# A four-layer vision kernel on one core: layer 3's bias tables built by DRAM-to-DRAM copies, and activation groups placed behind ready decays

## The chip, the cores and the metric

The kernel runs on one core of a Trainium2 chip. The metric is the device time of one execution in microseconds (us), lower is better. Engines are named as in the profile: PE (TensorE), DVE (VectorE), ACT (ScalarE), POOL (GpSimd) and SP (SyncE, which here only issues DMAs). Everything is fp32.

## The reference, cut to what matters

Four images of 64 x 64 positions and 128 channels go through four layers, image by image independently.

```python
# layer 0: state-space scan block (256 inner channels, 16 states, 4 directions)
xn = _ln(input); x_, z = split(xn @ in_proj_w)
xc = silu(depthwise_conv3x3(x_) + conv_b)
xs = stack([x0, x1, x0[..., ::-1], x1[..., ::-1]])       # rows, columns, and both reversed
delta = softplus(dts + dt_b); A = -exp(A_log)
h = exp(d_t * A) * h + (d_t * x_t) * B_t                  # scan over 4096 positions
y_t = einsum('bkdn,bkn->bkd', h, C_t)
x = input + (_ln(y) * silu(z)) @ out_proj_w
x = x + gelu(_ln(x) @ fc1_w + fc1_b) @ fc2_w + fc2_b
# layer 1: attention over all 4096 positions; layer 2: convolutions with hard-swish
# layer 3: attention of each position over its 7 x 7 neighbourhood, 4 heads
bias = rpb[:, rel_i][..., rel_j]
attn = softmax(einsum('nhijc,nhiajbc->nhijab', q, kwin) + bias)
x = x + attn_out @ proj_w + proj_b
x = x + gelu(_ln(x) @ fc1_w + fc1_b) @ fc2_w + fc2_b
```

## The kernel before, in words

**The scan.** `selective_scan` (L457 on) handles one image at a time: four directions, eight chunks of 512 positions, two halves, four groups of states, two pairs. The innermost step, a *unit*, works on a tile `[128, 2, 512]`. POOL makes `dB` = du x B (L504). For each of two halves g, ACT makes the decay `dA` = exp(delta x A) into a PSUM bank (L510; three banks in turn), and DVE scans along the positions (L512). The product with C (`hc`, into which PE sums at L558) is made by POOL for a fixed part of the units (L525; 5 of 16 for image 0, 7 of 16 for the others, `ON_POOL`), else by DVE in two halves (L517). There are 2048 units and so 4096 decays, 1024 to an image. The inputs `dt`, `du`, `b_rows` and `c_rows` come from DRAM through SP's queue, with four buffers each.

**What feeds it.** `scan_inputs` (L277) runs once for each image: LayerNorm, projection, the 3 x 3 convolution and silu chunk by chunk, then for both orders of positions the softplus on ACT and the product `du` on POOL (L328), all stored in DRAM. Image 0's inputs come first; those of images 1, 2 and 3 follow beside image 0's scan.

**What follows it.** `rest` runs the later stages of one image beside the scan of the next: `scan_output` (end of layer 0 with its MLP; its first product on DVE is `gated`, L626), `layer1`, `layer2` and `layer3_attention` (its product `oT` on DVE, L1387, comes once for each of eight chunks). The second half of layer 3, `layer3_mlp`, runs beside the next image's `scan_output`. Image 3's `rest` has the core to itself.

**What orders the work.** Nothing is ordered by hand. A scheduler puts each engine's instructions in an order when the kernel is built, by priorities and by its own estimate of when an instruction is ready; a lower number goes first. The scan has `SCAN_FIRST`, 10,000,000, and the other stages count up from zero, so they go ahead of it. On the chip each engine then keeps that order. SBUF pools are reused stack-wise: a stage that opens a pool waits until the memory's last user is done.

**Groups.** ACT's exp and ln share one function table; gelu and silu need others. The class `Together` (L100) puts the gelus or silus of one step in a row: each waits for the step's last matmul, all have a priority of -100 x `SCAN_FIRST`, and `exp_table` (L93) then loads the exp table back at once. There are 100 groups, of four activations nearly always.

**The bias tables.** `make_bias` (L1187) builds T, `[128, 52, 64]`: for each key column, head and row distance the bias at every query column, or -10000 outside of the window. It then builds 12 tables of 1 MB for three kinds of chunk. For each it fills a tile `bt` with -10000 on DVE (L1240), copies three or so row ranges out of T (L1251, SBUF to SBUF) and stores `bt` to DRAM (L1252). There is one `bt` buffer, so each memset waits for the store before it. The pool of T and `bt` is freed after that, and the scan inputs of image 1 use the memory next. `layer3_attention` loads the tables much later (L1325).

Of the kernel before, what the change touches and what calls it, by code (L numbers as in the profile page):

```python
# [28 lines left out]
F32 = mybir.dt.float32  # L29
# [14 lines left out]
NCH = NT // LC  # L44
# [10 lines left out]
BEHIND = 2  # L55
ON_POOL = ((1, 4, 7, 10, 13), (0, 2, 4, 6, 9, 11, 13))
SCAN_FIRST = 10_000_000

# [7 lines left out]
def mid(ap, n):  # L68

    return bc(ap.unsqueeze(1), [ap.shape[0], n, ap.shape[1]])  # L70
# [6 lines left out]
@contextmanager  # L77
def priority(tc, K, base):

    kept = tc.cur_priority  # L80
    tc.cur_priority = K.next_priority.get(base, base)
    yield
    K.next_priority[base] = tc.cur_priority
    tc.cur_priority = kept
# [15 lines left out]
class Together:  # L100
# [8 lines left out]
            after(self.tc, matmul, self.done)  # L109

    def run(self, last_matmul, acts):
        with priority(self.tc, self.K, -100 * SCAN_FIRST):
            for act in acts:
                self.done = act()
                after(self.tc, self.done, last_matmul)
        exp_table(self.tc, self.K, self.done)


# [941 lines left out]
def key_kind(c):  # L1060
    return 0 if c == 0 else 2 if c == NCH - 1 else 1
# [122 lines left out]
    nc.vector.tensor_scalar(K.bounds[0:1, 0, 7:8], top[:, 0:1], -1.0, 1.0, ALU.mult, ALU.add)  # L1184


def make_bias(tc, K, A, out):  # L1187

    nc = tc.nc
    NR = 2 * KW - 1
    NQ = 9
    with ExitStack() as ctx:
        pool = ctx.enter_context(tc.tile_pool(name="bias", bufs=1))
        psum = ctx.enter_context(tc.tile_pool(name="bias_p", bufs=4, space=PSUM))
        rp = loader(tc, pool, A, 3)("rpbT", [NR, HEADS * NR])

        shifted = pool.tile([NR, 2 * W], F32, name="shifted")
        nc.gpsimd.memset(shifted, 0.0)  # L1200
        nc.gpsimd.affine_select(
            shifted, shifted, [[1, 2 * W]], ALU.not_equal, 1.0, base=KW - W, channel_multiplier=-1
        )
        dist = pool.tile([128, W], F32, name="dist")
        kj = pool.tile([128, W], F32, name="kj")
        for i in range(2):
            half = slice(64 * i, 64 * i + 64)
            for t, pattern, base in ((dist, [[-1, W]], KW - 1), (kj, [[0, W]], 0)):
                nc.gpsimd.iota(
                    t[half, :], pattern, base=base, channel_multiplier=1, allow_small_or_imprecise_dtypes=True  # L1210
                )
        low = pool.tile([128, W], F32, name="low")
        high = pool.tile([128, W], F32, name="high")
        t = pool.tile([128, W], F32, name="t")
        nc.vector.tensor_scalar(low, dist, float(KW // 2), None, ALU.is_ge)
        nc.vector.tensor_scalar(t, kj, float(W - KW), None, ALU.is_ge)
        nc.vector.tensor_max(low, low, t)
        nc.vector.tensor_scalar(high, dist, float(KW - 1 + KW // 2), None, ALU.is_le)
        nc.vector.tensor_scalar(t, kj, float(KW - 1), None, ALU.is_le)
        nc.vector.tensor_max(high, high, t)  # L1220
        nc.vector.tensor_mul(low, low, high)
        nc.vector.tensor_scalar(low, low, -1.0, -FAR, ALU.add, ALU.mult)
        T = pool.tile([128, HEADS * NR, W], F32, name="T")
        for q0 in range(0, W, NQ):
            n = min(NQ, W - q0)
            ps = psum.tile([128, NQ, HEADS * NR], F32, name="ps")
            for q in range(n):
                first = W - 1 - q0 - q
                for i in range(2):
                    nc.tensor.matmul(  # L1230
                        ps[64 * i : 64 * i + 64, q, :], shifted[:, first : first + W], rp, start=True, stop=True
                    )
            nc.vector.tensor_add(
                T[:, :, q0 : q0 + n], ps[:, :n, :].rearrange("p q e -> p e q"), mid(low[:, q0 : q0 + n], HEADS * NR)
            )
        T4 = T.rearrange("p (h r) w -> p h r w", h=HEADS)
        for c in (0, 1, NCH - 1):
            for i, group in enumerate(key_groups(c)):
                bt = pool.tile([128, HEADS, RC, W], F32, name="bt")
                nc.vector.memset(bt, FAR)  # L1240
                for tile_, q0, q1, at in group:
                    for r in range(2):
                        key, half = 2 * tile_ + r, slice(64 * r, 64 * r + 64)
                        rows = [
                            q for q in range(q0, q1)
                            if 0 <= key - min(max(RC * c + q - KW // 2, 0), H - KW) < KW
                        ]
                        if rows:
                            n, to = len(rows), at + rows[0] - q0
                            far = KW - 1 - key + RC * c + rows[0]  # L1250
                            nc.sync.dma_start(bt[half, :, to : to + n, :], T4[half, :, far : far + n, :])  # L1251
                nc.sync.dma_start(out[key_kind(c)][i], bt.rearrange("p h r w -> p h (r w)"))  # L1252


def layer3_attention(tc, K, A, D, img, wide, out=None):
# [445 lines left out]
def network(tc, A, out):  # L1701
    nc = tc.nc
    with ExitStack() as ctx:
        nc.scalar.preload_act_table_set("natural_log_exp_and_others")
        K = make_consts(ctx, tc)
        dram = ctx.enter_context(tc.tile_pool(name="scratch", bufs=1, space=DRAM))

        def scratch(name, shape):
            return dram.tile(shape, F32, name=f"{name}_dram")

        D = SimpleNamespace()
        D.bias = scratch("bias", [len(BIAS_KINDS), 128, HEADS * 512])
        D.biasT = [[scratch(f"biasT{k}_{i}", [128, HEADS, LC]) for i in range(4)] for k in range(3)]
        D.conv_diag = scratch("conv_diag", [128, ND, 9, 128])
        D.w2_norms = scratch("w2_norms", [128, len(NORMS2), 4])
        D.w2_cv4, D.w2_bias = scratch("w2_cv4", [128, 128]), scratch("w2_bias", [1, 128])
        for name, shape in (("sz", [128, ND, LC]), ("xc", [128, ND, LC]), ("y", [128, ND, LC])):
            setattr(D, name, [[scratch(f"{name}{b}_{c}", shape) for c in range(NCH)] for b in range(B)])
        for name, shape in (("delta", [128, ND, LC]), ("du", [128, ND, LC]), ("bc", [NS, 2, LC])):
            made = [  # L1720
                [[scratch(f"{name}{b}_{k}_{c}", shape) for c in range(NCH)] for k in range(KD)] for b in range(B)
            ]
            setattr(D, name, made)
        D.y_first = [[[scratch(f"y_first{b}_{k}_{c}", [128, ND, LC]) for c in range(NCH)] for k in range(2)] for b in range(B)]
        D.y_cols = [scratch(f"y_cols{b}", [NCH, 128, NCH, ND, RC * RC]) for b in range(B)]
        for name in ("x4", "x5"):
            setattr(D, name, [scratch(f"{name}_{b}", [NT, C]) for b in range(B)])
        D.shift = [scratch(f"shift{b}", [NJ, 128]) for b in range(B)]

        with ExitStack() as scan_ctx:  # L1730
            S = make_scan(scan_ctx, tc, K, A)
            make_conv_diagonals(tc, K, A, D.conv_diag)
            with priority(tc, K, SCAN_FIRST // 2):
                with tc.tile_pool(name="mk_w2", bufs=1, side="right") as pool:
                    make_layer2(tc, K, A, D, pool)
            scan_inputs(tc, K, A, D, 0)
            before = None
            for img in range(B):
                with priority(tc, K, SCAN_FIRST):
                    selective_scan(tc, K, S, D, img)  # L1740
                if img == 0:
                    make_bias(tc, K, A, D.biasT)
                    for later in range(1, B):
                        scan_inputs(tc, K, A, D, later)
                    more = scan_ctx.enter_context(tc.tile_pool(name="ss_more", bufs=1))
                    S.products.widen(more, 4)
                    S.inputs.widen(more, 1)
                else:
                    rest(tc, K, A, D, img - 1, before)
                    before = img - 1, out[img - 1]  # L1750
            rest(tc, K, A, D, B - 1, before, scan_ctx.close, out[B - 1])
        needed = ctx.enter_context(tc.tile_pool(name="needed", bufs=1)).tile([1, 1], mybir.dt.int32, name="needed")
        bound_exceeded(tc, K, needed)
        with tc.If(nc.values_load(needed) > 0):
            everything_again(tc, K, A, D, out)
# [80 lines left out]
```

## Time and profile before

| what | us |
|---|---|
| median of three runs (lowest, highest) | 8791.7 (8789.48, 8803.95) |
| the profiled execution | 8797.75 |
| its span in the trace | 8795.8 |
| busy in the span: DVE, POOL, PE, ACT | 7141.1, 7049.4, 6999.8, 5683.3 |
| last decay (L510) starts | 7592.9 |
| first `gated` (L626) of image 3 | 7753.1 |

A line of groups gives source line, engine, operation, tiles (out<-in), shapes and count, then after the bar the busy time in us, the mean duration of one in ns, and after the next bar the time that the engine was idle just before them, with what ended it. A line of windows gives the stretch, its length, the busy us and instruction count of PE, PEld (weight loads), DVE, ACT and POOL, the granted PE clock, the share of the DMA engines' time that was busy, and GB/s. In the line of 40 slices each digit is a busy share in tenths.

### The profile page before, as it was taken

The numbers are of one execution on the slowest core, as the hardware profiler recorded it, in microseconds if no ns is written. First come the engines' busy times: TensorE is split into PE (matmuls) and PEld (weight loads), VectorE is DVE, ScalarE is ACT, GpSimd is POOL, SyncE is SP. The second block draws the span as 40 slices with busy tenths as digits, with TensorE's granted clock in tenths as the row PEclk, the third lists the DMA queues.
The fourth block names the chain that finished last, engine by engine and source line by source line (L and its number), as shares of the span: only waits on it lengthen the run. The fifth ranks groups of instructions, "written<-read, shape, count | busy, mean of one in ns | idle before, by whom it ended". The sixth has DMA issues, their size and how long they took to land. (4 is left out here: it accounts for less than half of the span.)

```text
span 8795.8 us, 102113 instructions
## 1 busy us (share of the span) xinstructions
PE 6999.8 (80%) x30532; PEld 2613.9 (30%) x30532; DVE 7141.1 (81%) x8531; ACT 5683.3 (65%) x11661; POOL 7049.4 (80%) x3079
## 2 busy tenths in 40 slices
PE   6844858687679897887789987777799888788988
PEld 2211313132332222333322222233322223344333
DVE  4789878787899999998899999998899999513433
ACT  5645767676566676666766676667766676454366
POOL 6888999989889999998899999998899999500000
PEclk8756868787789998898899988898899988899989
DMA  5777777777655556566555557565455565320020
GB/s 178 242 235 240 246 252 236 268 245 256 194 168 172 169 175 213 193 217 196 164 175 170 175 167 233 194 217 183 155 177 173 180 215 195 108 70 5 1 82 12
DMA packets 855473, 1572.02 MB, mean 179 GB/s; under 512 B 218341, under 2 KB 336764, under 8 KB 851197
## 3 DMA queue, kind: packets, MB, share of 16 engines
q1 hardware_dynamic: 724605, 1389.21, 48.1%
q10 hardware_dynamic: 130304, 176.19, 5.7%
q8 instruction: 244, 4.00, 0.2%
q14 instruction: 320, 2.62, 0.1%
HBM read 1273.92 MB, written 280.18 MB: 177 GB/s over the span
## 5 line engine op out<-in xcount | busy, mean ns | idle before, releaser
L504 POOL TENSOR_TENSOR dB<-du,b_rows 128x1024 f32<-128x1024 f32 x2048 | 4835.5, 2406 | 416.0 <-DVE hc L512 112.3
L510 ACT ACTIVATE dA<-dt,w_A_log 128x512 f32<-128x512 f32 x4096 | 2781.3, 690 | 481.7 <-DVE hc L512 217.8
L512 DVE TENSOR_TENSOR_SCAN dA<-dA,state,dB 128x512 f32<-128x512 f32 x2128 | 2629.6, 1272 | 273.8 <-POOL dB L504 134.9
L525 POOL TENSOR_TENSOR hc<-hc,c_rows 128x1024 f32<-128x1024 f32 x832 | 2003.9, 2409 | 64.4 <-ACT state L521 29.1
L512 DVE TENSOR_TENSOR_SCAN hc<-dA,state,dB 128x512 f32<-128x512 f32 x1456 | 1804.3, 1267 | 148.2 <-ACT dA L510 110.5
L517 DVE TENSOR_TENSOR hc<-dA,c_rows 128x512 f32<-128x512 f32 x2432 | 1563.6, 675 | 92.1 <-PE py L558 60.5
L558 PE MATMUL py<-hc,pick 128*32 128x512 f32 x8192 | 1231.5, 682 | 383.4 <-POOL hc L525 294.3
L519 ACT COPY state<-dA 128x1 f32<-128x1 f32 x2128 | 326.7, 159 | 1292.1 <-DVE hc L517 1281.8
L848 PE MATMUL pa<-e,l_v 128*128 128x512 f32 x2048 | 1061.4, 650 | 14.4 <-ACT e L804 12.5
L800 PE MATMUL pair<-l_g,l_f 32*128 32x512 f32 x2048 | 528.0, 664 | 169.9 <-ACT e L804 141.0
L988 POOL MEMSET l_h<- 64x128 f32 x8 | 2.1, 256 | 811.6 <-DVE l_h L962 811.6
L804 ACT ACTIVATE e<-pair 128x1024 f32<-128x1024 f32 (+1 forms) x448 | 508.4, 1135 | 221.0 <-PE pair L800 213.7
L848 PEld LDWEIGHTS pa<-e,l_v 128*128 128x128 f32 x2048 | 374.8, 199 | 666.1 <-issue 620.4
L558 PEld LDWEIGHTS py<-hc,pick 128*32 128x32 f32 x8192 | 209.9, 116 | 1148.2 <-issue 472.5
L247 PE MATMUL ps<-band,w_conv_diag 128*128 128x504 f32 (+3 forms) x1152 | 500.2, 594 | 6.0 <-ACT delta L397 5.6
L1354 PE MATMUL pair<-table,ident 128*128 128x512 f32 x768 | 400.4, 646 | 100.1 <-ACT e L1364 72.9
L512 DVE TENSOR_TENSOR_SCAN dA<-dA,dB 128x512 f32<-128x512 f32 x304 | 355.9, 1211 | 62.2 <-POOL dB L504 51.7
L201 PE MATMUL ps<-ident,ln_xn 128*128 128x128 f32 x512 | 136.5, 363 | 316.3 <-ACT ln_xn L198 251.6
L328 POOL TENSOR_TENSOR du<-delta,xc 128x1024 f32<-128x1024 f32 x128 | 334.6, 2622 | 56.6 <-ACT delta L397 50.1
L1364 ACT ACTIVATE e<-pair 128x1024 f32<-128x1024 f32 (+1 forms) x224 | 254.6, 1137 | 161.5 <-PE pair L1358 160.9
L247 PEld LDWEIGHTS ps<-band,w_conv_diag 128*128 128x128 f32 x1152 | 221.4, 193 | 285.0 <-issue 262.6
L800 PEld LDWEIGHTS pair<-l_g,l_f 32*128 32x128 f32 x2048 | 139.0, 188 | 518.7 <-ACT e L804 284.0
(285 smaller groups left out, 8709.7 us busy)
## 6 DMA issues: line engine op xcount, KB each, us to landing
b_rows<-bc_dram SPq DMA_DIRECT2D x1024, 256.0 KB
c_rows<-bc_dram SPq DMA_DIRECT2D x1024, 256.0 KB
dt<-delta_dram SPq DMA_DIRECT2D x512, 512.0 KB
du<-du_dram SPq DMA_DIRECT2D x512, 512.0 KB
delta_dram<-delta ACTq DMA_DIRECT2D x128, 512.0 KB
du_dram<-du SPq DMA_DIRECT2D x128, 512.0 KB
table<-biasT_dram SPq DMA_DIRECT2D x72, 512.0 KB
y_first_dram<-y_sum ACTq DMA_DIRECT2D x128, 256.0 KB
```

The source lines that it names most:

```text
L247: mm = nc.tensor.matmul(out[:, r0 - row0 : r1 - row0, c0:c1], lhsT((dy + 1) * 3 + dx + 1), src[:, r0 + dy : r1 + dy, c0 + dx : c1 + dx], s ...
L328: nc.gpsimd.tensor_mul(du.rearrange("p d (a b) -> p d a b", b=H), deltas[b].rearrange("p d (a b) -> p d a b", b=H), tk,)
L504: nc.gpsimd.tensor_mul(dB, dus[pp], mid(bt, 2))
L510: nc.scalar.activation(dA, dts[pp][:, g, :], AF.Exp, scale=S.A[:, k, j, pr, g : g + 1])
L512: nc.vector.tensor_tensor_scan(hg[:, order], dA[:, order], dB[:, g, order], 0.0 if i == 0 else state[:, j, pr, g : g + 1], ALU.mult, ALU.add,)
L517: mm = nc.vector.tensor_mul(hc[:, g, :], dA, ct)
L525: made.append(nc.gpsimd.tensor_mul(hc, hc, mid(ct, 2)))
L558: mm = nc.tensor.matmul(py[0][32 * q : 32 * q + 32, :], S.pick, hcs[q // 2][:, q % 2, :], start=(k == 1 and j == 0), stop=(j == NJS - 1),)
L800: nc.tensor.matmul(ps[:, u, :], f[quad, t // 4, span(t % 4, 128)], g[quad, c, :], start=True, stop=True)
L804: made = nc.scalar.activation(e, ps, AF.Exp)
L848: nc.tensor.matmul(pa, v[:, 8 * q + t, :], es[q], start=(t == 0 and q == 0), stop=(t == 7 and q == 3),)
L1354: nc.tensor.matmul(ps[:, u, :], K.ident, t[:, u, :], start=True, stop=False)
```

## The change

Two things. First, T gets one more row that holds -10000 throughout, and is stored to DRAM (`D.T`). The 12 tables are put together from there by DMAs whose source and destination are both in DRAM: one for each run of rows that follow each other in T, and one for each row that lies outside of the window. These DMAs are issued from `place_bias`, after the pool is closed and with the priority `LAST` x `SCAN_FIRST`, behind everything else. `bt`, its memsets and its copies are gone. Second, the first activation of a group gets that same last priority, and the others follow it with the old one.

```diff
+LAST = 50
...
     def run(self, last_matmul, acts):
-        with priority(self.tc, self.K, -100 * SCAN_FIRST):
-            for act in acts:
+        first = None
+        for act in acts:
+            with priority(self.tc, self.K, (LAST if first is None else -100) * SCAN_FIRST):
                 self.done = act()
                 after(self.tc, self.done, last_matmul)
+            if first is None:
+                first = self.done
+            else:
+                after(self.tc, self.done, first, mybir.DependencyClass.NoSync)
         exp_table(self.tc, self.K, self.done)
...
-def make_bias(tc, K, A, out):
+def make_bias(tc, K, A, D):
...
-        T = pool.tile([128, HEADS * NR, W], F32, name="T")
+        T = pool.tile([128, HEADS * NR + 1, W], F32, name="T")
+        nc.vector.memset(T[:, HEADS * NR, :], FAR)
...
-        T4 = T.rearrange("p (h r) w -> p h r w", h=HEADS)
-        for c in (0, 1, NCH - 1):
-            for i, group in enumerate(key_groups(c)):
-                bt = pool.tile([128, HEADS, RC, W], F32, name="bt")
-                nc.vector.memset(bt, FAR)
...
-                            nc.sync.dma_start(bt[half, :, to : to + n, :], T4[half, :, far : far + n, :])
-                nc.sync.dma_start(out[key_kind(c)][i], bt.rearrange("p h r w -> p h (r w)"))
+        nc.sync.dma_start(D.T, T)
+    with priority(tc, K, LAST * SCAN_FIRST):
+        place_bias(tc, D)
+
+
+def place_bias(tc, D):
+
+    NR = 2 * KW - 1
+    T4 = D.T[:, : HEADS * NR, :].rearrange("p (h r) w -> p h r w", h=HEADS)
+    for c in (0, 1, NCH - 1):
+        for i, group in enumerate(key_groups(c)):
+            out = D.biasT[key_kind(c)][i].rearrange("p h (r w) -> p h r w", w=W)
+            for r in range(2):
+                half = span(r, 64)
+                rows = [None] * RC
                 for tile_, q0, q1, at in group:
...
+                    key = 2 * tile_ + r
+                    for q in range(q0, q1):
+                        if 0 <= key - min(max(RC * c + q - KW // 2, 0), H - KW) < KW:
+                            rows[at + q - q0] = KW - 1 - key + RC * c + q
+                first = 0
+                while first < RC:
+                    n = 1
+                    if rows[first] is None:
+                        src = bc(D.T[half, HEADS * NR :, :], [64, HEADS, W])
+                        tc.nc.sync.dma_start(out[half, :, first, :], src)
+                    else:
+                        while first + n < RC and rows[first + n] == rows[first] + n:
+                            n += 1
+                        src = T4[half, :, rows[first] : rows[first] + n, :]
+                        tc.nc.sync.dma_start(out[half, :, first : first + n, :], src)
+                    first += n
...
+        D.T = scratch("T", [128, HEADS * (2 * KW - 1) + 1, W])
...
-                    make_bias(tc, K, A, D.biasT)
+                    make_bias(tc, K, A, D)
```

More of the change, by code (lines that the diff above doesn't have):

```diff
@@ L1233, in make_bias @@
             nc.vector.tensor_add(
-                T[:, :, q0 : q0 + n], ps[:, :n, :].rearrange("p q e -> p e q"), mid(low[:, q0 : q0 + n], HEADS * NR)
+                T[:, : HEADS * NR, q0 : q0 + n], ps[:, :n, :].rearrange("p q e -> p e q"), mid(low[:, q0 : q0 + n], HEADS * NR)
             )
-        T4 = T.rearrange("p (h r) w -> p h r w", h=HEADS)
-        for c in (0, 1, NCH - 1):
-            for i, group in enumerate(key_groups(c)):
-                bt = pool.tile([128, HEADS, RC, W], F32, name="bt")
-                nc.vector.memset(bt, FAR)
-                for tile_, q0, q1, at in group:
[L1242 to L1250, printed above, removed]
-                            nc.sync.dma_start(bt[half, :, to : to + n, :], T4[half, :, far : far + n, :])
-                nc.sync.dma_start(out[key_kind(c)][i], bt.rearrange("p h r w -> p h (r w)"))
```

## The prediction

> **What bounds the kernel now.** I read the busy shares in 40 slices first: they part the span into a scan stage and a tail. Line L510, the decay `dA`, runs 4096 times (1024 for each image, in image order), so I use "decay n" of ScalarE's order as a clock that can be read in both kernels.
>
> ```profile
> DVE  4789878787899999998899999998899999513433
> ACT  5645767676566676666766676667766676454366
> POOL 6888999989889999998899999998899999500000
> ...
> DMA  5777777777655556566555557565455565320020
> ```
>
> POOL and DVE are near full until slice 34 (7600 us). ScalarE is at six tenths, so it is not the bound, though it can block DVE for some us. Second, the costliest groups.
>
> ```profile
> L504 POOL TENSOR_TENSOR dB<-du,b_rows 128x1024 f32<-128x1024 f32 x2048 | 4835.5, 2406 | 416.0 <-DVE hc L512 112.3 <-DVE dA L512 89.2 <-issue 67.3
> L510 ACT ACTIVATE dA<-dt,w_A_log 128x512 f32<-128x512 f32 x4096 | 2781.3, 690 | 481.7 <-DVE hc L512 217.8 <-DVE hc L517 186.9 <-ACT state L519 6.6
> ...
> L517 DVE TENSOR_TENSOR hc<-dA,c_rows 128x512 f32<-128x512 f32 x2432 | 1563.6, 675 | 92.1 <-PE py L558 60.5 <-DMA c_rows<-bc_dram 19.1 <-PE ps L354 0.4
> ...
> L1240 DVE MEMSET bt<- 128x2048 f32 x12 | 21.2, 1765 | 12.8 <-DMA biasT_dram<-bt 4.8 <-DMA du<-du_dram 2.0 <-ACT dA L510 1.9
> ```
>
> A unit (two decays) costs DVE two scans of about 1.27 us, and two products of 0.675 us unless POOL takes the product. For image 0 POOL takes 5 of 16: DVE needs (11 x 3.89 + 5 x 2.53)/16 = 3.47 us a unit, POOL 21 x 2.36/16 = 3.10. DVE is the bound there unless the `du` products of the scan inputs (2.6 us each, L328) load POOL. For images 1 to 3 it is 7 of 16: DVE 3.29, POOL 23 x 2.41/16 = 3.46, so POOL is the bound. Third, the windows of 50 us (PE, PEld, DVE, ACT, POOL, clock, DMA share, GB/s).
>
> ```profile
> 450.00:500.00 50.00, 28.00 (x77) 6.73 (x76) 37.79 (x40) 30.07 (x68) 50.00 (x21) 0.60 0.73 253
> ...
> 600.00:650.00 50.00, 15.48 (x58) 1.93 (x58) 46.87 (x49) 18.58 (x30) 40.57 (x18) 0.53 0.86 252
> 650.00:700.00 50.00, 11.38 (x48) 1.40 (x48) 46.76 (x50) 22.49 (x53) 41.77 (x19) 0.50 0.86 265
> 700.00:750.00 50.00, 11.80 (x52) 1.42 (x56) 47.12 (x49) 21.85 (x51) 40.32 (x18) 0.50 0.84 258
> ```
> ```profile
> 7550.00:7600.00 50.00, 36.08 (x201) 13.95 (x200) 45.01 (x54) 27.60 (x49) 45.38 (x20) 0.83 0.24 79
> 7600.00:7650.00 50.00, 36.75 (x250) 15.64 (x246) 2.52 (x10) 12.86 (x22) 0.00 (x0) 0.86 0.07 19
> 7650.00:7700.00 50.00, 42.23 (x269) 19.64 (x268) 0.94 (x2) 13.32 (x15) 0.00 (x0) 0.97 0.28 85
> 7700.00:7750.00 50.00, 32.22 (x168) 12.87 (x168) 2.87 (x7) 7.37 (x8) 0.00 (x0) 0.82 0.22 63
> ```
>
> With `du` on POOL (450) POOL is full. While the bias is made (600 to 750) DVE is full and POOL idles a fifth. After the last decay (7592.9) come 160 us in which only PE works: the rest of image 2's attention. Only then does image 3's scan_output begin (its first `gated` starts at 7753). I call these 160 us the overhang; they are a cost of image 2's stages being late against the scan.
>
> **The change part by part.**
>
> *The memsets.* Twelve memsets of `bt`, 12 x 1.765 = 21.2 us, go from DVE in the stretch where DVE is the bound; with them the waits before them of 1.6, 2.3, 2.5 and 2.0 us (gaps over 0.8 us in the timeline, two of them for a landing of `biasT_dram<-bt`), about 8. The new memset of one row of T is 64 elements wide: nothing. -29 us, bounds -21 and -34 (all 12.8 us of idle).
>
> *The start of image 1's scan inputs.* They no longer wait for the bias tiles. In the changed kernel's instruction order their first silu group stands at decay 239, not 339. The three images' inputs take as many decays in both orders (702, from 339 to 1041; 706, from 239 to 945), so the hundred decays with nothing beside them go from ahead of the inputs to behind them, and image 0's own stages begin at decay 961 instead of 1055. Some 63 decays of scan_output now meet image 0's mix, where DVE is the bound: 1.74 us a decay plus some 50 us of gated, LayerNorm and residual work on DVE over 140 decays (0.35) is 2.09, and before they ran at 2.02 a decay (290.5 us for 144). Equal within 5 us. I take 0, bounds -15 and +15.
>
> *The overhang.* All three images' later stages follow one another without a gap, so the lead is handed on, though it shrinks: the `oT` products (L1387) of image 2 stand at decays 3894, 3937, 3982, 4031, 4078, then three after the last decay, before; 3850, 3903, 3952, 4001, 4045, 4091, then two, after. On the chip the sixth came at 7633.4, 40.5 us after the last decay; now it is 5 decays ahead of it (5 x 1.69 = 8 us): 49 us. The second count agrees: behind the last decay the order has 115 matmuls fewer (2728 to 2613), 230 records; 7600 to 7750 holds 687 records, 4.6 a us: 50 us. From there on every engine's order is the same to the end, so the tail gives nothing else. -48, bounds -25 (the scan ends earlier by the memsets, the attention does not) and -60.
>
> *The copies.* Gone are 36 copies T to `bt` (11.0 MB) and 12 stores of 1 MB; new are one store of T (1.7 MB) and 57 copies from DRAM to DRAM, 12.6 MB, of 256 packets each. They all stand between decay 226 and 263, some 68 us, mixed with 33 regular loads on SP's one queue. What is queued behind a copy is the next `b_rows`, `c_rows`, `dt` or `du`, for which POOL and ACT wait. By the packets of the trace (256 B 18 ns, 1792 B 126, 2048 B 84 to 100; 256 B the same in stores of `y_cols` to DRAM as in loads from it) the copies take 50 us of all 16 engines, T's store some 7. The plain stretch had a regular share of 0.45 (31 us), and the inputs' weights of 1.9 MB add 9: 97 us in 68, 29 late. Four buffers of `b_rows`, one per four decays, are loaded some 21 us ahead. 8 us are left; the queue is uneven, so I take +12. No row shows a copy from DRAM to DRAM. Lower bound 0; upper bound +36: if both sides count as traffic, 38.5 MB at the most that any window moved (309 GB/s, 1600 to 1650) is 125 us, less 68 and 21.
>
> The Trainium skill (DMA: Bandwidth & Descriptors, Specifications) gives an HBM limit of about 358 GB/s for a core; with both sides counted that is an estimated 108 us instead of 125, so +19 instead of +12 and a sum 7 us higher. The same table asks for 512 B at least for line rate, and 27 of the 57 copies move 256 B; the trace agrees in part: 18 ns for 256 B, 27 for 512.
>
> *The groups of gelus and silus.* A group is a table load of 1.283 us (L226 or L359), four activations and the load back (L96): 5.0 us; in the timeline DVE idles 2.9 us around each of the 74 groups of the scan stage, 214 us in all. Putting a group behind ready decays would help if decays were ready when it starts. But at its start on the chip all three `dA` banks were already made and not yet freed in 60 of 74 groups, and two in the other 14 (decays begun less the DVE instructions that free a bank). The orders say the same: banks made and not yet freed where a group stands are 3, 2, 1, 0 in 38, 18, 15, 3 groups before, in 39, 16, 14, 5 after. So 0; bounds -20 (14 groups, 1.4 us each) and +15.
>
> **Sum.** -29 + 0 - 48 + 12 + 0 = -65 us. The profiled execution took 8797.75 us (span 8795.8 and 2 us around it), so 8733; it lies 6 us over the median of the runs shown (8791.7), so I forecast **8727**.
>
> **Rivals.**
>
> *The queue jams.* SP issues a copy of 256 packets in 0.63 us when the queue is free, up to 1.98 when it is not (L1251). If a copy costs B us in the queue, the loads behind are late by 57 B + 13 - 68 - 21. The sum turns slower by over 0.2% when that passes 95 us, so from B = 3.0; with B = 4 the loads are 152 us late: 8727 - 12 + 152 = 8867. For it: `bt` copies of 448 KB took 2.7 to 3.9 us from first packet to last, beside others, and DMA was already at 0.86. Against it: several run at once, 256 KB took 1.2 to 2.6, and nearly half the copies are 64 KB. Chance 0.09.
>
> *The scan gives the lead back.* With the earlier stages on image 0's DVE-bound mix, each of the 63 decays pays 0.35 us (22 us) instead of using POOL's idle time, the copies cost their 36, and image 2's attention gains only 25: -29 + 22 - 25 + 36 = +4, 8796; by halves 8775. Chance of the neighbourhood of no change 0.14.
>
> *The groups do get cover.* If the count of the 14 groups is worth its full 20 us and the silus in the inputs get a bank more, 8707 or a little below. Against it stands the unchanged count. Chance 0.12.
>
> *The forecast*, 8700 to 8774: 0.65.
>
> **Range and chances.** Low: the two gains at full with the groups' 20 and no copies, -34 - 60 - 20 = -114, 8678. High: the second rival, 8796. Range 8678 to 8796; what is left out is the jam and the ends. A difference under 0.2% (18 us) can't be told from none here. Faster 0.77, same 0.14, slower 0.09.
>
> **What would show each step.** The windows between decays 226 and 263 (some 583 to 650 us) should show a DMA share near 1 and POOL gaps for `b_rows` of some 10 us in all; over 80 us of them is the jam. L1240 is gone, and L188 (bn_stats of image 1) starts near 600, not 777 us. The last decay should come about 17 us earlier (7576), and the first `gated` of image 3 some 112 us behind it instead of 160; from there to the end 1043 us as before. DVE's idle time around a group should stay at 2.9 us; at 1.5 the groups' part was underrated. If the last decay comes no earlier but the overhang shrinks, the copies ate the memsets' gain. The forecast is wrong if the pace in stages that I took as unchanged (1.65 to 1.69 us a decay beside attention) moves by even 1%: that is 40 us.

## The result, and the profile after

The changed kernel takes 8780.3 us (median of 19 runs, 8760.7 to 8785.3); the kernel before, run beside it, took 8795.7 (19 runs). The ratio is 0.9976, interval [0.997, 0.9983]: 15 us faster, where 65 were forecast. The profiled span is 8778.8 us against 8795.8. I split it, as the prediction did, at the last decay and at the first `gated` of image 3:

| | last decay | overhang | tail | span |
|---|---|---|---|---|
| before | 7592.9 | 160.2 | 1042.7 | 8795.8 |
| forecast | 7576 | 112 | 1043 | 8731 |
| after | 7623.6 | 117.6 | 1037.7 | 8778.8 |

The overhang did what was foreseen. The last decay went the other way: 31 us later instead of 17 earlier. Line numbers after the change are 6 higher: L504, L510, L512 and L517 of before are L510, L516, L518 and L523. The slices of the page after:

```profile
DVE  4788788888899999988899999988899999713433
ACT  5657676675666676667766666667766666554366
POOL 6888989898899999988899989988899989700000
...
DMA  5776767776455566565454555665455565420020
```

The DMA row hardly moves. POOL's row has a 9 in 18 of the 34 slices of the scan, where before it had one in 23. The costliest groups say it as a sum:

```profile
L510 POOL TENSOR_TENSOR dB<-du,b_rows 128x1024 f32<-128x1024 f32 x2048 | 4800.4, 2370 | 444.0 <-DVE hc L518 112.4
...
L518 DVE TENSOR_TENSOR_SCAN hc<-dA,state,dB 128x512 f32<-128x512 f32 x1456 | 1803.3, 1267 | 186.2 <-ACT dA L516 138.6
L523 DVE TENSOR_TENSOR hc<-dA,c_rows 128x512 f32<-128x512 f32 x2432 | 1561.8, 675 | 118.7 <-PE py L564 86.5
```

The same scan in the kernel before:

```profile
L512 DVE TENSOR_TENSOR_SCAN hc<-dA,state,dB 128x512 f32<-128x512 f32 x1456 | 1804.3, 1267 | 148.2 <-ACT dA L510 110.5
```

The work is the same to a per cent (POOL's `dB` is even 35 us shorter), but POOL's idle time before it rose from 416 to 444 us, and DVE's before this scan from 148 to 186. Over all scans together the traces put 236 us of DVE's idle time down to a decay of ScalarE before and 308 after, and 221 and 176 down to POOL's `dB`. So the scan is not doing more; it is standing still longer, and what it stands still for is a decay from ScalarE.

The windows where the copies were expected, and those round the last decay (columns as before):

```profile
600.00:650.00 50.00, 36.97 (x116) 14.24 (x116) 41.80 (x59) 32.79 (x70) 37.95 (x17) 0.84 1.02 342
...
7600.00:7650.00 50.00, 38.98 (x200) 14.70 (x200) 28.00 (x38) 21.60 (x38) 26.09 (x12) 0.76 0.14 46
7650.00:7700.00 50.00, 44.26 (x304) 20.50 (x304) 1.37 (x2) 12.48 (x13) 0.00 (x0) 1.00 0.25 80
```

A DMA share of 1.02 at 600 is the forecast "near 1", and POOL (last busy column) idles 12 us there. At 7600 DVE and POOL are still half busy, where before they had stopped. The copies by their tile (minimum, median, maximum ns of one issue, first and last start), and what POOL waited for from 578 to 660 us:

```profile
L1273 SPq DMA_DIRECT2D biasT_dram<-T_dram x33: 520/603/1156, 581.2 to 655.1; - x33
L1268 SPq DMA_DIRECT2D biasT_dram<-T_dram x24: 520/595/1153, 583.2 to 653.2; - x24
```
```profile
POOL dB L510 <- DMA T_dram<-T: 7.8, 1, 7.8
...
POOL dB L510 <- DMA biasT_dram<-T_dram: 4.5, 2, 3.6
```

There was no jam: an issue took 0.6 us, POOL's waits put down to the copies are 4.5 us, and ScalarE's 2.8. The 7.8 us put down to T's store are not the store's: the kernel before has no such store, and POOL waits as long at the same place there, for a scan of DVE:

```profile
POOL dB L504 <- DVE dA L512: 14.9, 6, 7.8
```

That is less than the 12 us that the sum had for the copies. So the 48 us that are missing are not here, and the question for the experiments was where in the scan they went.

### The profile page after: what moved, and what is told of

Same layout as the page of the kernel before. It is cut to its first block, busy times and chain, and to the rows that moved or that the text cites. A ratio compares the mean times of both kernels' runs of the same rounds, so it can differ in the third digit from the quotient of the medians.

```text
span 8778.8 us, 102147 instructions
## 1 busy us (share of the span) xinstructions
PE 7039.8 (80%) x30532; PEld 2636.3 (30%) x30532; DVE 7111.7 (81%) x8520; ACT 5677.5 (65%) x11661; POOL 7046.7 (80%) x3079
## 5 line engine op out<-in xcount | busy, mean ns | idle before, releaser
L510 POOL TENSOR_TENSOR dB<-du,b_rows 128x1024 f32<-128x1024 f32 x2048 | 4800.4, 2370 | 444.0 <-DVE hc L518 112.4
L516 ACT ACTIVATE dA<-dt,w_A_log 128x512 f32<-128x512 f32 x4096 | 2778.8, 690 | 464.0 <-DVE hc L518 201.6
L518 DVE TENSOR_TENSOR_SCAN dA<-dA,state,dB 128x512 f32<-128x512 f32 x2128 | 2627.9, 1272 | 291.8 <-POOL dB L510 146.0
L531 POOL TENSOR_TENSOR hc<-hc,c_rows 128x1024 f32<-128x1024 f32 x832 | 1972.2, 2370 | 69.4 <-ACT state L527 24.6
L518 DVE TENSOR_TENSOR_SCAN hc<-dA,state,dB 128x512 f32<-128x512 f32 x1456 | 1803.3, 1267 | 186.2 <-ACT dA L516 138.6
L523 DVE TENSOR_TENSOR hc<-dA,c_rows 128x512 f32<-128x512 f32 x2432 | 1561.8, 675 | 118.7 <-PE py L564 86.5
L518 DVE TENSOR_TENSOR_SCAN dA<-dA,dB 128x512 f32<-128x512 f32 x304 | 357.5, 1211 | 45.0 <-ACT dA L516 28.5
```

What stands on the lines that cost most here:

```text
L510: nc.gpsimd.tensor_mul(dB, dus[pp], mid(bt, 2))
L516: nc.scalar.activation(dA, dts[pp][:, g, :], AF.Exp, scale=S.A[:, k, j, pr, g : g + 1])
L518: nc.vector.tensor_tensor_scan(hg[:, order], dA[:, order], dB[:, g, order], 0.0 if i == 0 else state[:, j, pr, g : g + 1], ALU.mult, ALU.add,)
L523: mm = nc.vector.tensor_mul(hc[:, g, :], dA, ct)
L531: made.append(nc.gpsimd.tensor_mul(hc, hc, mid(ct, 2)))
```

## The experiments

All ratios are to the kernel before, run on the same chip. "POOL idle" is POOL's idle time in the three stretches of scan_output that lie beside the scan, each from its first `gated` to layer 1's first `l_f`. The times are medians; the last decay, the overhang and the idle times are those of one profiled execution, which for e1 was 14 us longer than its median.

| kernel | us | ratio [95%] | last decay | overhang | POOL idle |
|---|---|---|---|---|---|
| before (profiled span) | 8795.8 | | 7592.9 | 160.2 | 184 |
| after | 8780.3 | 0.9976 [0.997, 0.9983] | 7623.6 | 117.6 | 218 |
| e1 bias part alone | 8734.9 | 0.9929 [0.9916, 0.9943] | 7625.3 | 71.5 | 214 |
| e2 groups part alone | 8799.9 | 1.0002 [0.9993, 1.0011] | 7601.3 | 159.0 | 181 |
| e3 after, copies twice | 8702.3 | 0.9893 [0.9878, 0.9908] | 7631.1 | 28.4 | 213 |
| e4 bias alone, copies out of SBUF | 8761.8 | 0.9963 [0.9949, 0.9976] | 7619.3 | 95.0 | 215 |
| e5 bias alone, inputs held | 8801.7 | 1.0005 [0.9996, 1.0014] | 7587.5 | 172.6 | 188 |
| e6 bias alone, tables after inputs 3 | 8694.2 | 0.9883 [0.9868, 0.9898] | 7601.0 | 55.9 | 207 |
| e7 bias alone, tables after inputs 1 | 8688.5 | 0.9875 [0.986, 0.989] | 7594.1 | 55.7 | 210 |
| e8 after, inputs held | 8840.4 | 1.0045 [1.0031, 1.0059] | 7598.8 | 200.9 | 205 |
| e9 before, no gelus and silus | 8743.9 | 0.9936 [0.992, 0.9953] | 7549.4 | 164.3 | 131 |
| e10 bias alone, no gelus and silus | 8561.3 | 0.973 [0.9713, 0.9746] | 7506.0 | 18.0 | 133 |

**The two parts by themselves.** e1 is the changed kernel with the old `run` of `Together`; e2 the kernel before with the new one.

```diff
 # e1, against after
-        first = None
-        for act in acts:
-            with priority(self.tc, self.K, (LAST if first is None else -100) * SCAN_FIRST):
+        with priority(self.tc, self.K, -100 * SCAN_FIRST):
+            for act in acts:
                 self.done = act()
                 after(self.tc, self.done, last_matmul)
-            if first is None:
-                first = self.done
-            else:
-                after(self.tc, self.done, first, mybir.DependencyClass.NoSync)
 # e2 is the reverse: before, with after's run() and LAST
```

> The bias part of the change alone: the tables by copies from DRAM to DRAM, the groups of gelus and silus as before. Theory G (the missing 50 us were lost in the groups: the first gelu, put behind everything, also lets LayerNorm work of ScalarE go ahead of it, so that no decay is made for longer; VectorE's idle time around the 40 gelu groups grew): VectorE idles about 2.9 us around a group again, the scan_output stretches run at 2.02 us a decay, and the time is 8730 to 8755. Theory S (what is moved beside the scan costs the scan what it gains behind it, whatever the groups do): the last decay comes later still, since here the order puts more of image 2's attention ahead of it (the sixth oT at decay 4059), the overhang is near 100 us, and the time stays at 8770 to 8790.

> The groups' part of the change alone, on the kernel before with its bt tiles. Theory G: slower than before by 20 to 50 us, if the groups lose by themselves. Theory S, and the instruction order (the stages stand at the same decays as before, and ScalarE has 77 other instructions in the gaps around the gelu groups instead of 73): within 10 us of before, 8785 to 8805; then the groups' loss in the changed kernel comes only from where its stages stand.

The late last decay comes with the bias part (7625 in e1, 7601 in e2), and with the old groups of e1 DVE idles 3.7 us around a group, as in after. So theory G, which put the loss into the groups, falls, though e1's 8735 us lie in its range. S, that work moved beside the scan costs the scan, is right on the last decay; it missed the time (8770 to 8790), and does not say how. By itself the groups part does nothing. Beside the bias part it costs 45 us, and the profiles show it in the overhang (71.5 to 117.6): in the instruction order the first `oT` of image 2 stands at decay 3827 in e1 and at 3850 in after, so the order with new groups is 23 decays late. e5 and e8 differ in the same way (3905 and 3919; 39 us). Why the scheduler's order loses these decays with the one and not with the other kernel was not found.

**The copies.** e3 issues each copy a second time, into DRAM that nobody reads. e4 takes them out of the tile T instead of `D.T`, which also drops T's store and starts the inputs at decay 274 instead of 239.

```diff
 # e3, against after, behind each copy (one of two shown)
+                        tc.nc.sync.dma_start(again[half, :, first : first + n, :], src)
 # e4, against e1, cut to the source
-    T4 = D.T[:, : HEADS * NR, :].rearrange("p (h r) w -> p h r w", h=HEADS)
+    T4 = T[:, : HEADS * NR, :].rearrange("p (h r) w -> p h r w", h=HEADS)
```

> The changed kernel with every DRAM-to-DRAM copy issued twice, the second time into other DRAM that nobody reads (114 copies between decays 226 and 291). If the copies cost the scan the 17 us by which the first stretch of image 1's inputs ran slower: that stretch loses 15 to 30 us more, and the pool waits for b_rows and c_rows there double. If the copies hide: under 5 us more there. What the later stages do is another matter, since their order shifts.

> As the bias part alone, but the 57 copies read T in SBUF, so T is not stored and the memory is held until they are done: image 1's inputs start at decay 274 instead of 239. If the DRAM-to-DRAM copies cost something in themselves (12 us in the forecast), this is 5 to 15 us faster than the bias part alone in the stretch from decay 226 to 600; if only the early start costs, it lies between before and the bias part alone; if neither costs, it equals the bias part alone less the memory's delay (35 decays later).

Another 57 copies moved the last decay from 7623.6 to 7631.1, and the end of the inputs from 2083.3 to 2089.7. But 7 us is not the price of a set. Counted from image 1's first silu group (decay 239 in both), e3 is 26 us behind the changed kernel 60 decays later, and 36 behind 160 decays later. Neither expectation was met: POOL's waits put down to copies did not double (0.9 us, 4.5 in after), but from 575 to 800 us ScalarE's waits put down to DMAs are 32 us, against 3. By the end of the inputs all but 6 us were made good; how was not followed. For one set, e6 and e7 (below) give the price, since their inputs start with no copies beside them: counted from the first silu group, the changed kernel is never more than 9 us behind them in 160 decays, and 1 to 2 us behind at the end of these.

The surprise is the total: with 57 useless copies more the kernel is 78 us *faster* than after, because the overhang fell to 28 us: the scheduler's order came out otherwise (first `oT` at 3793 instead of 3850). e4 has no DRAM-to-DRAM copy, and POOL's idle time in scan_output is as high as in e1; from decay 226 to 600 it takes 746 us and e1 748, so no cost of copying out of DRAM shows there, though e4's inputs start 35 decays later. Its time lies between before and e1, as was expected if only the early start costs. The DRAM-to-DRAM copies are not the loss.

**The place of scan_output.** In every kernel with the bias part so far scan_output begins some 60 to 100 decays earlier than before. e5 and e8 undo that alone: image 1's first input load waits for decay 326.

```diff
 # e5 against e1, e8 against after
+                            K.decays += 1
+                            if K.decays == HOLD:          # HOLD = 326
+                                K.held = decay
...
+                if img == 1 and c == 0 and not K.general:
+                    after(tc, load_x, K.held)
```

> The bias part alone (groups as before); the first load of image 1's scan inputs waits for decay 326, so the inputs begin at decay 335 instead of 235 and image 0's scan_output at decay 1055, where it stood in the kernel before, instead of 961; the copies stay. The runs so far: POOL idle in the three stretches of scan_output 184 us in the kernel before, 213 to 218 in all four kernels with the bias part; last decay 7593 before, 7619 to 7631 with it. Theory P (the earlier place of scan_output against the scan costs the scan those 30 us): POOL idle there falls back to about 184, the last decay comes at about 7580 (7593 less the memsets, plus the copies), the first gated of image 3 some 170 us behind it (first oT at decay 3905 in the order; 3894 gave 160), tail 1042, so 8790. Theory Q (the loss comes from something else in the bias part, and the place is innocent): POOL idle stays at some 215, last decay at 7615 to 7625, and with the same 170 us the time is about 8830.

> The changed kernel with both parts, and the same wait for decay 326 ahead of image 1's scan inputs: scan_output at 1055, 2071, 3155, first oT of image 2 at decay 3919, only four of the eight before the last decay. Theory P: POOL idle in scan_output about 184 us, last decay about 7580, overhang about 190, tail 1038: 8808. Theory Q: last decay 7620, same overhang: 8848. By either it is slower than the kernel before, where the change held its lead back.

e5 is by theory P in its three terms (POOL idle 188, last decay 7587.5, overhang 172.6), with a total 12 us above P's. e8 is between the theories (last decay 7599, POOL idle 205), and slow because it lost the lead (overhang 201). The early start was thus what made the loss, all of it in e5 and 25 of 31 us of the last decay in e8, and also what made the gain: with the inputs held the bias part alone is back at the time of before. But it didn't say yet whether the place acts by itself. The lines below are the sums of the windows of the three stretches (sum of the lengths, then busy PE, PEld, DVE, ACT, POOL), of before, after, e1 and e5 in this order:

```profile
sum 1117.70, PE 854.20 PEld 434.18 DVE 984.05 ACT 819.53 POOL 934.08; mean PE 284.73 PEld 144.73 DVE 328.02 ACT 273.18 POOL 311.36
```
```profile
sum 1157.40, PE 876.88 PEld 451.16 DVE 990.51 ACT 818.01 POOL 939.42; mean PE 292.29 PEld 150.39 DVE 330.17 ACT 272.67 POOL 313.14
```
```profile
sum 1156.80, PE 872.92 PEld 435.32 DVE 987.56 ACT 816.18 POOL 942.44; mean PE 290.97 PEld 145.11 DVE 329.19 ACT 272.06 POOL 314.15
```
```profile
sum 1142.70, PE 860.70 PEld 431.76 DVE 1004.34 ACT 828.25 POOL 954.50; mean PE 286.90 PEld 143.92 DVE 334.78 ACT 276.08 POOL 318.17
```

Take POOL from the first number: 183.6, 218.0, 214.4, 188.2 us idle. From before to after DVE and POOL did 5 to 6 us more work in 40 us more time.

**Another place for the tables.** e6 calls `make_bias` after the inputs of image 3, e7 after those of image 1; both have the old groups.

```diff
-                    make_bias(tc, K, A, D)
                     for later in range(1, B):
                         scan_inputs(tc, K, A, D, later)
+                        if later == 1:                   # e7
+                            make_bias(tc, K, A, D)
+                    make_bias(tc, K, A, D)               # e6
```

> The bias part alone, and the tables are made after the scan inputs of image 3 instead of ahead of those of image 1: T's DVE work and the copies stand at decays 955 to 995, the inputs begin at 217, image 0's scan_output at 957. First oT of image 2 at decay 3803 in the order, as with the doubled copies, where the overhang was 28 us. Theory P: scan_output is as early as in the bias part alone (957 against 961), so POOL's idle time there stays at some 215 us and the last decay at 7615 to 7630; overhang 28, tail 1045: 8690 to 8705. Theory Q (the loss comes from the bias work done early, ahead of the inputs): POOL idle falls to some 184, the last decay to about 7590, and with the same overhang 8665.

> The bias part alone, with the tables made between the scan inputs of image 1 and those of image 2: copies at decays 469 to 509, inputs from 217, scan_output at 967, 1983, 3049; first oT of image 2 at 3803. Theory P: POOL idle in scan_output some 215 us, last decay 7615 to 7630, overhang 28, tail 1045: 8690 to 8705, the same as with the tables made after image 3's inputs. If the place of the copies matters by itself (beside inputs, where the DMA engines' share is 0.73, or behind them), this kernel and that one differ by more than 15 us in POOL's idle time up to the end of the inputs.

Here theory P misses on the last decay: scan_output is as early as in e1 (957 and 967), yet the last decay is 24 and 31 us earlier than there, and POOL idle is 207 and 210. The overhang came out at 56, not 28: I had taken it from e3, whose first `oT` in the order stands ten decays earlier (3793 against 3803). From the first decay to the end of the inputs POOL idles 170 us in e6, where the copies come behind this stretch, and 173 in e7, where they lie in it; so the place of the copies does not matter. Over the plain pace of the scan (1.635 us a decay, worked out below) the three scan_outputs cost 224 and 231 us here, 215 in before and 249 in e1. So the place of scan_output alone does not set the loss. These are the fastest kernels that compute everything, 104 and 109 us under before.

**What the scan stands still for.** I then measured every stretch of ScalarE between two decays that holds a group of gelus (40 of them; all lie in scan_output). DVE's idle time and its stage work (`gated`, LayerNorm, residual) are counted from the end of the decay ahead to 0.5 us past the end of the decay behind.

| us | before | after | e1 | e3 | e4 | e5 | e6 | e7 | e8 |
|---|---|---|---|---|---|---|---|---|---|
| ScalarE makes no decay, 40 groups | 241 | 263 | 251 | 246 | 240 | 230 | 242 | 231 | 245 |
| DVE's stage work meanwhile | 17 | 15 | 14 | 9 | 8 | 14 | 16 | 12 | 12 |
| DVE idle | 104 | 133 | 135 | 124 | 122 | 101 | 115 | 115 | 117 |
| first row less the two others | 121 | 116 | 103 | 114 | 109 | 115 | 111 | 103 | 116 |
| the three scan_outputs over 1.635 a decay | 215 | 248 | 249 | 241 | 249 | 217 | 224 | 231 | 227 |

The fourth row is what DVE still does for the scan on decays that are already made, 2.6 to 3.0 us a group; stage work adds 0.2 to 0.4. DVE's idle time is the time without a decay less these two, and it goes with the cost of scan_output in the last row. From before to after it rises by 29 us: 22 of longer stretches without a decay, 5 of less work on ready decays, 2 of less stage work. In e1 it rises by 32, of which 19 are less work on ready decays: when a gelu group starts, all three banks hold a decay that is made in 29 groups of before and two in the other 11; in e1 it is three in 24, two in 12 and one in 4. Two groups show both ends. In before, at decay 3217, the timeline of DVE (start, duration, work, and the idle time before it):

```profile
6064.02 2.46 DVE L512 TENSOR_TENSOR_SCAN dA<-dA,state,dB 128x512 f32<-128x512 f32 x2
6066.38 1.62 DVE L188 BATCH_NORM_STATS2 ln_stats<-x 128x6 f32<-128x128 f32 x8
6067.92 1.27 DVE L517 TENSOR_TENSOR hc<-dA,c_rows 128x512 f32<-128x512 f32 x2
6069.10 0.63 DVE L190 BATCH_NORM_AGGREGATE ln_mv<-ln_stats 128x2 f32<-128x6 f32 x8
6069.66 1.26 DVE L512 TENSOR_TENSOR_SCAN dA<-dA,state,dB 128x512 f32<-128x512 f32 x1
6070.95 0.69 DVE L517 TENSOR_TENSOR hc<-dA,c_rows 128x512 f32<-128x512 f32 x1
6072.46 1.29 DVE L512 TENSOR_TENSOR_SCAN dA<-dA,state,dB 128x512 f32<-128x512 f32 x1 [0.82 <-ACT dA L510]
```

In after, at decay 2012, first ScalarE, then DVE:

```profile
3946.80 0.84 ACT L200 ACTIVATE ln_shift<-ln_mv,ln_less 128x1 f32<-128x1 f32 x4
3947.66 1.28 ACT L232 ACT_TABLE_LOAD   x1
3948.95 2.42 ACT L232 ACTIVATE mlp_h<-ps,w_fc_b 128x512 f32<-128x512 f32 x4
3951.39 1.28 ACT L97 ACT_TABLE_LOAD   x1
...
3952.74 0.85 ACT L200 ACTIVATE ln_shift<-ln_mv,ln_less 128x1 f32<-128x1 f32 x4
3953.49 1.64 ACT L204 ACTIVATE ln_xn<-x,ln_shift,ln_rstd 128x128 f32<-128x128 f32 x4
...
3955.16 1.30 ACT L516 ACTIVATE dA<-dt,w_A_log 128x512 f32<-128x512 f32 x2
```
```profile
3947.92 1.26 DVE L518 TENSOR_TENSOR_SCAN hc<-dA,state,dB 128x512 f32<-128x512 f32 x1
3949.11 0.35 DVE L196 BATCH_NORM_AGGREGATE ln_mv<-ln_stats 128x2 f32<-128x6 f32 x4
3955.94 2.47 DVE L518 TENSOR_TENSOR_SCAN dA<-dA,state,dB 128x512 f32<-128x512 f32 x2 [6.49 <-issue]
```

ScalarE is without a decay for 8.6 us in the first (6063.1 to 6071.7) and 8.4 in the second. In the first, statistics of a LayerNorm and the scans fill it, and DVE loses 0.82 us; in the second ScalarE does LayerNorm work ahead of the group and behind it, DVE has one scan and one aggregate to do, and loses 6.49. Theory L is that the loss is this and nothing else: how long the order keeps ScalarE from the decays at a group, and how much it leaves DVE to do meanwhile.

e9 and e10 test it. They leave out the gelus and silus (Identity in their place) in before and in the bias part alone, so that a group takes 2.4 us of ScalarE instead of 5.0 and the order has little left to make worse.

```diff
 # e9 against before, e10 against e1
-            lambda f=f: nc.scalar.activation(hT[:, f, :], phs[f], AF.Gelu, bias=P.b1[:, f : f + 1])
+            lambda f=f: nc.scalar.activation(hT[:, f, :], phs[f], AF.Identity, bias=P.b1[:, f : f + 1])
...
-        exp_table(self.tc, self.K, self.done)
```

> The kernel before with the gelus and silus left out: each is an Identity activation from the same PSUM to the same tile, and the table loads of the groups are gone, so a group takes some 2.5 us of ScalarE instead of 5.0. It is the partner of the next kernel; scan_output stands at 1055, 2075, 3145 as before. Theory L (the scan stops at a group for as long as ScalarE makes no decay, less the work that DVE happens to have then; the loss of the bias part is more of these stops): DVE's idle time in the 74 decay gaps with a group falls from 211 us to under 80, the last decay from 7593 to some 7450, overhang 160, tail 1000 to 1035: 8630.

> The bias part alone with the gelus and silus left out in the same way. scan_output at 938, 1970, 3031, so even earlier than with gelus (961, 1993, 3067). Theory L: without long groups there is little left that the order can make longer, so the last decay comes earlier than in its partner by what the memsets give less what the copies take, 15 to 30 us (7425 or so), and POOL's idle time in scan_output is within 10 us of the partner's. Theory P (an earlier place of scan_output costs the scan by itself): POOL's idle time there is again some 30 us higher and the last decay comes 15 to 30 us later than the partner's (7470 or so). Overhang by the first oT at decay 3781: some 20 to 30; time by L 8480, by P 8530.

The sums of the same three stretches, e9 and then e10:

```profile
sum 1033.60, PE 828.07 PEld 425.21 DVE 958.85 ACT 700.93 POOL 902.76; mean PE 276.02 PEld 141.74 DVE 319.62 ACT 233.64 POOL 300.92
```
```profile
sum 1006.50, PE 822.53 PEld 420.26 DVE 941.62 ACT 685.55 POOL 873.40; mean PE 274.18 PEld 140.09 DVE 313.87 ACT 228.52 POOL 291.13
```

POOL idles 130.8 and 133.1 us: the 31 us between e1 and before are down to 2, though scan_output now stands even earlier (938, 1970, 3031). And the last decay of the bias part comes 43 us earlier than its partner's, not 32 later. L holds and P falls: an early place costs nothing when no long group is there to be met badly. Two sizes were off. The total of e9 stayed at 8744 where 8630 was expected: the last decay fell by 43 us only. DVE's idle time at all 74 groups fell from 211 to 116 us, not under 80: at the gelu groups from 104 to 35, but at the silu groups only from 107 to 81, and the scan inputs became no shorter. And the 43 us of gain are more than the 15 to 30 expected.

## Why the prediction was wrong

To see each term I took from each stage's time 1.635 us for each decay that runs in it. That is the plain pace of the scan: e5 has 96 decays more than e1 ahead of the inputs, with nothing beside them, and takes 157.0 us longer. What is left is what the other stages cost the scan:

| us over 1.635 a decay | before | after | e1 | e5 | e9 | e10 |
|---|---|---|---|---|---|---|
| up to image 1's inputs | 144 | 118 | 116 | 116 | 150 | 112 |
| the three inputs | 277 | 297 | 295 | 275 | 273 | 281 |
| the three scan_outputs | 215 | 248 | 249 | 217 | 157 | 148 |
| layers 1 to 3 | 160 | 166 | 171 | 186 | 178 | 173 |
| sum | 797 | 829 | 832 | 794 | 759 | 714 |

*The memsets, -29:* right. The first row shows -28 in e5, with the copies in it, which run there without inputs beside them.

*The copies, +12:* too much, though within the bounds. The waits put down to them are 7 us, and against e6 and e7 the changed kernel is at most 9 us late in the first 160 decays of the inputs, and 1 to 2 at their end. Their packets took some 40 us of all 16 engines, an estimate from the mean times between 581 and 662 us, where 50 were forecast (1792 B took 87 ns, and 126 in the copies into `bt`). The first two rows together still give -6.6 after the change, where -17 was forecast. The 20 us that the three inputs lost are not the copies' for the most part: e6's inputs meet none and cost 288 us in that row, and its first 160 decays from the first silu group take 316 us, as after's do (317; before 297). The rise goes with DVE's idle time at the 34 silu groups of the inputs, from 107 to 142 us (134 in e6); that link is argued, no run tried it. The rival of the jammed queue is out: an issue took 0.6 us, and all 57 left the queue in 74 us, 1.3 us each, not the 3 from which it would have decided.

On the copies the prediction quoted the Trainium skill (DMA: Bandwidth & Descriptors, Specifications) with about 358 GB/s for a core and took both sides of a copy as traffic. From 578 to 660 us the trace has 25.9 MB, of which the copies are 12.6; with their second side that is 38.5 MB in 82 us, 469 GB/s. So that limit, counted with both sides, did not hold here; the trace decides, and the estimate of +19 by the page was worse than the +12.

*The overhang, -48:* right, -43. Reading it from the instruction order of the changed kernel worked, since that order already held the 23 decays that the groups part takes away again.

*The groups, 0:* right alone (e2), and the idle time round a group was the right thing to watch: it rose from 2.9 to 3.7 us over all 74 groups. But the rise is in e1 as well, with the old groups (3.7). The edit did not make it. What the groups part costs beside the bias part, 45 us, went through the order, which the term of the overhang had read.

*The early start, "I take 0, bounds -15 and +15":* this is the step that failed. It gave +33 us in the three stretches of scan_output. The working priced the 63 decays of scan_output that now meet image 0's mix, found 2.09 us a decay against 2.02 before, and called the stages equal. The pace was even right (306.5 us for 147 decays, 2.085), but it was only 9 us of the loss; 13 and 11 came in image 1's and 2's scan_output, where the mix has nothing to do with it. What the step had not priced is that about half of what scan_output costs the scan (104 of 215 us before, 133 of 248 after) lies in the stops at its gelu groups, and that these depend on what the scheduler puts there; they make 29 of the 33 us. Moving a stage by a hundred decays draws that anew, for all stages behind it: at nearly the same places the three scan_outputs cost 249 us in e1 and 224 in e6. The prediction named the exposure itself (1% of pace, 40 us), but held the paces fixed in its range of 15 us.

*The rivals.* "The scan gives the lead back", by halves 8775, has the right time and direction by luck, and the wrong mechanism: it put 22 us into image 0's mix and 36 into the copies, and let the overhang shrink by 25; the runs show 9, at most 9, and 43. Groups that get cover did not come about.

*Open.* Why one order makes the stops at the groups longer than another follows no rule that I found: with the bias part DVE's idle time at gelu groups is 101 to 135 us in eight orders. e5 also pays 26 us more than before in layers 1 to 3, which I have not followed up.

## What to carry to other kernels

Where a scheduler fixes the order, an edit that moves a stage is two edits: its own cost, and a new draw of the order behind it, worth plus or minus 30 to 50 us in this kernel; put the second into the range, and look for the kernel with the better draw (here, with the old groups, the tables made one stage later: 8688 us instead of 8735). Price a stage beside a scan by its stops, not by its mean pace: for each stretch in which the feeding engine does something else, its length less the fed engine's work on what is ready, less the other work that it has at that moment (here 2.6 to 3.0 and 0.2 to 0.4 us a group). Split the time at the last instruction of the scan and read lead from the order; that part of the forecast held.

## What the runs showed of the hardware

Copies from DRAM to DRAM were cheaper than feared: 57 of them, 12.6 MB, went out in 74 us with the DMA engines at 0.98 to 1.02 and the regular loads between them, and the scan was at most 9 us late against e6 and e7 in the first 160 decays of the inputs. Another 57 right behind them made it 36 us later for a time (e3). Where they ran in a stretch without inputs, copies out of SBUF were no cheaper than out of DRAM (the time over 1.635 us a decay up to the end of the inputs is 392 us in e4, 391 in e5).

A switch of ScalarE's function table costs 1.28 us and nothing more here: in the timeline above the gelus start 0.01 us after the load's end, and a whole group with two loads takes 5.02 us (median of 100 groups in before and in after). The Trainium skill (ScalarE: Activation LUTs, What ACT_TABLE_LOAD costs) counts a drain of about 1.38 us on top; by that, an estimate, a group would be some 2.8 us longer, and the trace does not show it.
